# Layer 0 attention of a two-layer network on one Trainium2 core: the first steps and the loop over tiles issued in written order, with the weight rounding's loads in buffers of their own

## The chip, the cores and the metric

The kernel runs on one core of one Trainium2 chip. A core has a tensor engine for matmuls (PE, which loads the stationary operand through a side queue, PEld), a vector engine (DVE), a scalar engine (ACT), a third elementwise engine (POOL, GpSimd) and a queue that only issues transfers (SP). Each takes its instructions strictly in the order of its own queue and waits for the others by semaphores. The metric is the device time of one execution in microseconds (us). The kernel before took 1146.04 us, the median of three runs (1140.92 to 1151.8).

## The reference, cut to what matters

Two layers, each a cross attention and a feed-forward part, over 8 sequences of 256 tokens of width 512, so 2048 tokens, which the kernel handles as 16 tiles of 128. Only layer 0's attention is edited, and the preparation of the weights of the layer 0 feed-forward part that runs beside it. All of it is f32 until the rounding:

```python
# layer 0 attention; x is the layernormed input, k = v = ctx
Q, K, V = (einsum('bshd,hde->bshe', t, Wh) for t in (xh, kh, vh))      # 4 heads of 128
scores  = einsum('bshe,bthe->bhst', Q, K) / sqrt(hd)
A       = maximum(abs((scores * decay).sum(axis=0)), 1.0)              # summed over the batch
O       = einsum('hst,bthe->bshe', A, V)
Y       = (O - mu) / sqrt(var + GN_EPS) * gn_gamma + gn_beta
x       = x + relu(xn @ wg_w) * Y @ wo_w
# layer 0 feed-forward: weights are rounded to -1, 0, 1
def weight_quant(w):
    scale = 1.0 / clip(mean(abs(w)), EPS)
    return clip(round(w * scale), -1.0, 1.0) / scale
```

Since A sums over the whole batch, no tile of O can begin before every tile's scores are in. Since a weight's scale is a mean over the whole matrix, no piece of it can be rounded before all its pieces were summed.

## The kernel before, in words

`layer0_attention` has two loops.

The first, over `n` (21 steps), normalizes one token tile per step: `stats` (DVE mean and variance, ACT square root), `normed` (DVE reciprocal and scaling, four PE transposes into bank "t", ACT copy to xnT). Four steps behind it follows `queries` (one PE matmul with G = Wh Whᵀ per head and chunk, DVE copy to q), and a step later `scores`, which add up in four PSUM banks "s0" to "s3". `values` (four matmuls into bank "pv", ACT copy to v) comes in the first four steps. WhT and G are made ahead of the loop, with ACT copies. `ternary.add` loads one of twelve weight pieces (704 KB each for w1 and w3, 768 or 512 KB for w2) and sums its absolute values on ACT (L166) into `part`.

The second loop, over `i` (16 tiles and one step more), does per tile:

- `attended` (L348, L351): eight matmuls with A and V into po; a layernorm of it (DVE L71, L73, ACT root L75, DVE L77, L78); POOL multiplies by gamma and adds beta (L354, L355);
- `centered`: loads a tile of ctx (raw) and subtracts each head's mean (DVE L334, L335, POOL L336, L337), then writes it to vc_d for layer 1;
- `turned` of the tile before: four transposes of wy into bank "t", ACT copy to wyT (L365);
- `gated`: DVE product of relu(pw) and y (L360); `gate` of the next tile (L316): four matmuls into pw;
- `output` of the tile before: four matmuls with wo (L371), DVE add into X (L372) and its statistics (L100, L101);
- for odd tiles up to 11, two `values` blocks (L250, L255) of a later sequence; for the last two tiles the input of the feed-forward part (`ffn_input`: ACT L421 and L407, DVE L402 to L425);
- `ternary.round`: ACT turns the piece rounded in the step before into bf16 (L182), a new piece is loaded (L156), ACT adds the magic number that rounds it (L191), DVE clips it (L192). Ahead of a weight's first piece, `scale` sums `part` over the partitions with one matmul into wtot, in bank "t", and DVE makes the scale from it (L173 to L176).

Both kinds of weight loads, for `add` and for `round`, share one tag "wst" with two buffers. Of the eight PSUM banks, "s0" to "s3" serve sums, then po and pz; "pq" has two, "t" and "pv" one each.

The order of the work is not the written one: a planner orders each engine's queue from the written program by priorities and a cost model and hands out buffers as they come free; a buffer is reused after all who read it. Elsewhere in the kernel (layer 1's attention) a block under `manual_schedule` keeps the written order on the engines that it names.

In the built program the planner has put all twelve sums of weight pieces ahead of or among tile 0's and tile 1's work on ACT, rounds pieces in pairs, and put each odd tile's second value block between the two halves of the next tile's `attended`.

Of the kernel before, what the change touches and what calls it, by code (L numbers as in the profile page):

```python
# [19 lines left out]
F32 = mybir.dt.float32  # L20
# [4 lines left out]
AF = mybir.ActivationFunctionType  # L25
# [5 lines left out]
P = 128  # L31
D = 512
# [7 lines left out]
H0 = 4  # L40
# [63 lines left out]
def transpose_blocks(g, pool, src, n, dtype, ident, tag):  # L104

    pt = pool.tile([P, n, P], dtype, tag=tag, name="pt")
    for k in range(n):
        g.nc.tensor.transpose(pt[:, k, :], src[:, k * P : (k + 1) * P], ident)
    return pt
# [22 lines left out]
class TernaryWeights:  # L132
# [5 lines left out]
    def __init__(self, g, pool, stage, ps):  # L138
        self.g, self.stage, self.ps = g, stage, ps
        g.wq, g.iw = [], g.const.tile([P, 3], F32, tag="iw", name="iw")  # L140
        self.pieces, self.sc = [], []
        for n, (src, kb, cols) in enumerate(((g.w1T, KD, FF), (g.w3T, KD, FF), (g.w2T, NF, D))):
            g.wq.append(pool.tile([P, kb, cols], BF16, tag=f"wq{n}", name=f"wq{n}"))
            step = self.COLS // cols
            of = [(n, src, a, min(a + step, kb), cols) for a in range(0, kb, step)]
            self.pieces.append(of)
            self.sc.append(g.const.tile([P, 1], F32, tag=f"wsc{n}", name=f"wsc{n}"))
        self.part = stage.tile([P, 3, KD], F32, tag="wpart", name="wpart", bufs=1)
        g.nc.vector.memset(self.part, 0.0)
        self.to_add = [(p, m) for of in self.pieces for m, p in enumerate(of)]  # L150
        self.to_round = list(self.to_add)
        self.clipped = []

    def load(self, n, src, a, z, cols):
        w = self.stage.tile([P, self.COLS], F32, tag="wst", name="wst", bufs=2)[:, : (z - a) * cols]
        self.g.nc.sync.dma_start(  # L156
            out=w.rearrange("p (k f) -> p k f", f=cols), in_=src.rearrange("(k p) f -> p k f", p=P)[:, a:z]
        )
        return w

    def add(self):

        if self.to_add:
            piece, m = self.to_add.pop(0)
            w = self.load(*piece)
            self.g.nc.scalar.activation(w, w, AF.Abs, accum_out=self.part[:, piece[0], m : m + 1])  # L166

    def scale(self, n):
        nc, g = self.g.nc, self.g
        tot = self.ps.tile([P, KD], F32, tag="t", name="wtot", bufs=1)  # L170
        nc.tensor.matmul(tot, lhsT=g.ones[:, :P], rhs=self.part[:, n], start=True, stop=True)
        mean = g.small.tile([P, 1], F32, tag="wmean", name="wmean")
        nc.vector.tensor_reduce(mean, tot, AX.X, ALU.add)  # L173
        nc.vector.tensor_scalar(mean, mean, 1.0 / (D * FF), 1e-5, ALU.mult, ALU.max)
        nc.vector.reciprocal(self.sc[n], mean)
        nc.vector.reciprocal(g.iw[:, n : n + 1], self.sc[n])  # L176

    def round(self):

        nc, g = self.g.nc, self.g  # L180
        for (n, _, a, z, _), w in self.clipped:
            nc.scalar.activation(  # L182
                g.wq[n][:, a:z].rearrange("p k f -> p (k f)"), w, AF.Identity, bias=g.eps["-magic"]
            )
        self.clipped = []
        if self.to_round:
            piece, m = self.to_round.pop(0)
            if m == 0:
                self.scale(piece[0])
            w = self.load(*piece)  # L190
            nc.scalar.activation(w, w, AF.Identity, bias=g.eps["magic"], scale=self.sc[piece[0]])  # L191
            nc.vector.tensor_scalar(w, w, MAGIC - 1.0, MAGIC + 1.0, ALU.max, ALU.min)  # L192
            self.clipped = [(piece, w)]


def layer0_attention(g, tc, cp, qpool):
# [7 lines left out]
    with ExitStack() as ctx:  # L204
# [28 lines left out]

        WhT = work.tile([P, H0, HD0], F32, tag="wyT", name="WhT")
        nc.scalar.copy(WhT, transpose_blocks(g, ps, Wh.rearrange("p h e -> p (h e)"), H0, F32, g.ident, "t"))
        pG = ps.tile([P, H0, HD0], F32, tag="pv", name="pG")
        for h in range(H0):
            nc.tensor.matmul(pG[:, h], lhsT=WhT[:, h], rhs=WhT[:, h], start=True, stop=True)  # L240
        G = wp.tile([P, H0, HD0], F32, tag="G", name="G")
        nc.scalar.copy(G, pG)

        V = {}

        def values(b, j):
            c, o = divmod(b * S + j * P, CH)
            pv = ps.tile([P, D], F32, tag="pv", name="pv")
            for h in range(H0):
                nc.tensor.matmul(  # L250
                    pv[:, h * HD0 : (h + 1) * HD0], lhsT=g.ctxT[c][:, h, o : o + P], rhs=Wh[:, h, :],
                    start=True, stop=True,
                )
            vj = work.tile([P, D], F32, tag=f"v{j}", name=f"v{j}")
            nc.scalar.copy(vj, pv)  # L255
            V.setdefault(b, []).append(vj)
# [8 lines left out]
        for h in range(H0):  # L265
            nc.tensor.matmul(sums[h], lhsT=zero[:, :P], rhs=zero, start=True, stop=False)
# [28 lines left out]

        of, q = {0: stats(0)}, {}
        for n in range(NT + H0 + 1):
            if n + 1 < NT:  # L300
                of[n + 1] = stats(n + 1)
            if n < NT:
                normed(n, *of.pop(n))
            if 0 <= n - H0 < NT:
                q[n - H0] = queries(*divmod(n - H0, H0))
            if 0 <= n - H0 - 1:
                scores(*divmod(n - H0 - 1, H0), q.pop(n - H0 - 1))
            if n < 4:
                values(*divmod(n, 2))
            elif n >= 6:  # L310
                ternary.add()
        def gate(i):
            c, o = divmod(i * P, CH)
            pw = ps.tile([P, D], F32, tag="pq", name="pw", bufs=2)
            for k in range(KD):
                nc.tensor.matmul(  # L316
                    pw, lhsT=xnT[c][:, k, o : o + P], rhs=wg[:, k, :], start=k == 0, stop=k == KD - 1
                )
            return pw

        pw = gate(0)
        for h in range(H0):
            nc.vector.tensor_mul(AT[h], sums[h], AT[h])
            nc.scalar.activation(AT[h], AT[h], AF.Abs)
            nc.vector.tensor_scalar(AT[h], AT[h], 1.0, None, ALU.max)

        def centered(i):


            raw = work.tile([P, D], F32, tag="raw", name="raw")  # L330
            nc.sync.dma_start(out=raw, in_=g.ctx[i * P : (i + 1) * P, :])
# [26 lines left out]
        def gated(pw, y):  # L358
            wy = work.tile([P, D], F32, tag="wy", name="wy")
            nc.vector.scalar_tensor_tensor(wy, pw, 0.0, y, ALU.max, ALU.mult)  # L360
            return wy

        def turned(wy):
            wyT = work.tile([P, KD, P], F32, tag="wyT", name="wyT")
            nc.scalar.copy(wyT, transpose_blocks(g, ps, wy, KD, F32, g.ident, "t"))  # L365
            return wyT
# [6 lines left out]
            norm_stats(g, g.mv[:, i, :], g.X[i])  # L373


        wy = {}
        for i in range(NT + 1):
            if i < NT:
                y = attended(i)
                centered(i)  # L380
            if i:
                wyT = turned(wy.pop(i - 1))
            if i < NT:
                wy[i] = gated(pw, y)
            if i + 1 < NT:
                pw = gate(i + 1)
            if i:
                output(i - 1, wyT)
            if NT - 2 <= i < NT:
                g.begun.append(ffn_turned(g, *ffn_input(g, work, i - NT + 2)))  # L390
            if i % 2 and i // 2 + 2 < B:
                for j in range(2):
                    values(i // 2 + 2, j)
            ternary.round()


def quantize(g, out, tmp, x):
# [1108 lines left out]
```

## Time and profile before

| what | value |
|---|---|
| median of three runs | 1146.04 us (1140.92 to 1151.8) |
| profiled execution, its own time | 1145.64 us |
| its span | 1143.8 us |
| PE / DVE / ACT / POOL busy | 1033.5 / 545.4 / 413.3 / 375.8 us |
| layer 0 attention, last output matmul ends | 238.5 us |
| PE busy in 0:20, 60:80, 120:140 us | 12.38, 13.87, 14.81 us |
| PE busy in 140:220 us | 80.00 us |
| granted PE clock, mean | 0.969 |

The span is from the first to the last instruction of one profiled execution; the time also holds what lies around it, 1.8 us here. Busy time is the union of an engine's instructions. A row of the timeline reads: start, duration, engine, line, operation, output tile and input tiles with shape, how many instructions are merged in the row, and in brackets how long the engine had been idle and what ended that idle time. An f32 matmul stands in the trace as two passes, so "x8" is four matmuls. Names are the program's tiles with the buffer number left out.

### The profile page before, as it was taken

To read this page: it belongs to the slowest core of one execution; us is meant where nothing else is said; L and a number is where in the kernel's file an instruction comes from. 1 tells how busy PE (TensorE), PEld (TensorE's weight loads), DVE (VectorE), ACT (ScalarE), POOL (GpSimd) and SP (SyncE) were. 2 spreads that over 40 slices of the span, in tenths; PEclk is the share of its full clock that TensorE was granted. 3 is DMA by queue.
4 is the path that set the end of the run, shared out by engine and by line. 5 is a ranking of instruction groups with operands and counts; after the bars stand their busy time and mean duration, and the time that the engine had idled before them with its cause. 6 is when DMAs were issued, how large, how long until landed. Compare 5 with 4: busy or idle time off the path is not lost. (4 is left out here: it accounts for less than half of the span.)

```text
span 1143.8 us, 14661 instructions
## 1 busy us (share of the span) xinstructions
PE 1033.5 (90%) x5207; PEld 617.6 (54%) x5222; DVE 545.4 (48%) x1443; ACT 413.3 (36%) x701; POOL 375.8 (33%) x347
## 2 busy tenths in 40 slices
PE   7979899989999688998898989999999999999994
PEld 5746466534444254555534435555556666667672
DVE  6545645568888637988836941121221121221210
ACT  4445424155675357578641002112122222111111
POOL 0144422220000001354651033444454555444422
PEclk9989899999999799899899989999999999999997
DMA  9776311023323111221022345767777777888872
GB/s 350 266 262 219 127 56 46 5 50 64 58 52 65 47 34 42 71 72 57 37 96 61 138 149 151 182 171 182 180 190 191 196 197 201 208 227 230 222 186 35
DMA packets 100483, 153.65 MB, mean 134 GB/s; under 512 B 38600, under 2 KB 41288, under 8 KB 100376
## 3 DMA queue, kind: packets, MB, share of 16 engines
q1 hardware_dynamic: 81488, 106.94, 30.2%
q0 software_dynamic: 18672, 45.58, 18.2%
q8 instruction: 43, 0.70, 0.3%
q14 instruction: 40, 0.33, 0.1%
q10 hardware_dynamic: 240, 0.10, 0.0%
HBM read 111.24 MB, written 33.49 MB: 127 GB/s over the span
## 5 line engine op out<-in xcount | busy, mean ns | idle before, releaser
L1314 POOL DMA_INDIRECT out_x<-eo,to x84 | 129.8, 1545 | 226.9 <-ACT eo L1340 212.0
L1254 PE MATMUL pg<-xT,w 128*128 128x288 f32 (+7 forms) x512 | 140.3, 417 | 3.9 <-DVE xT L1311 3.9
L1270 PE MATMUL po<-w,act 128*128 128x512 f32 (+3 forms) x448 | 139.6, 494 | 4.3 <-DVE act L1259 3.9
L1254 PE MATMUL pu<-xT,w 128*128 128x288 f32 (+7 forms) x512 | 136.7, 410 | 0.0
L1340 ACT ACTIVATE eo<-po,slotw 128x512 f32<-128x512 f32 (+3 forms) x112 | 64.5, 581 | 159.2 <-PE po L1270 156.8
L1258 ACT ACTIVATE sg<-pg 128x288 f32<-128x288 f32 (+8 forms) x68 | 29.0, 427 | 257.1 <-PE pg L1254 251.7
L1254 PEld LDWEIGHTS pg<-xT,w 128*128 128x128 f32 x512 | 95.3, 191 | 33.9 <-DVE xT L1311 7.2
L1254 PEld LDWEIGHTS pu<-xT,w 128*128 128x128 f32 x512 | 97.2, 190 | 29.1 <-issue 3.0
L1311 DVE COPY xT<-pt 128x512 f32<-128x512 f32 (+3 forms) x84 | 48.8, 618 | 132.8 <-PE pt L1310 118.3
L1305 DVE SCALAR_TENSOR_TENSOR of<-xg,is_rank 128x32 f32<-128x32 f32 (+3 forms) x84 | 15.8, 188 | 188.8 <-DMA xg<-h_d,tok_of 188.2
L1295 POOL DMA_INDIRECT xg<-h_d,tok_of x84 | 82.6, 983 | 64.9 <-DVE act L1259 37.0
L1270 PEld LDWEIGHTS po<-w,act 128*128 128x128 f32 (+3 forms) x448 | 55.5, 161 | 79.8 <-issue 50.0
L556 PE MATMUL p<-wq,xqT 128*128 128x512 bf16 (+1 forms) x379 | 79.5, 361 | 3.0 <-DMA xqT<-xq 2.0
L754 DVE SCALAR_TENSOR_TENSOR ct<-pqk,xe 128x768 f32<-128x768 f32 x64 | 58.3, 950 | 25.3 <-ACT xe L731 11.8
L316 PE MATMUL pw<-wg,xnT 128*128 128x512 f32 x128 | 61.5, 626 | 0.0
L556 PEld LDWEIGHTS <-xqT 128*128 128x128 bf16 x384 | 36.7, 98 | 44.1 <-DMA xqT<-xq 6.3
L371 PE MATMUL pz<-wo,wyT 128*128 128x512 f32 x128 | 57.8, 594 | 1.4 <-ACT wyT L365 1.4
L1310 PE MATMUL pt<-ident,xg 128*128 128x128 f32 (+4 forms) x336 | 46.0, 269 | 11.6 <-DVE xT L1311 10.0
L731 ACT ACTIVATE xe<-pd 128x512 f32<-128x512 f32 x96 | 54.1, 599 | 4.9 <-PE pd L727 4.6
L1259 DVE TENSOR_TENSOR act<-pu,sg 128x288 f32<-128x288 f32 (+8 forms) x68 | 32.0, 475 | 42.8 <-PE pu L1254 42.1
L1310 PEld LDWEIGHTS pt<-ident,xg 128*128 128x128 f32 (+4 forms) x336 | 35.0, 140 | 31.3 <-issue 17.5
L812 POOL TENSOR_TENSOR hid<-hid,rsq 128x1024 f32<-128x1024 f32 x8 | 15.3, 1913 | 105.3 <-PE pqk L750 79.2
(287 smaller groups left out, 1704.9 us busy)
## 6 DMA issues: line engine op xcount, KB each, us to landing
w<-in_w SPq DMA_DIRECT2D x32, 1024.0 KB
w<-in_w SPq DMA_DIRECT2D x32, 512.0 KB
wst<-in_w1T SPq DMA_DIRECT2D x8, 704.0 KB
wst<-in_w3T SPq DMA_DIRECT2D x8, 704.0 KB
wst<-in_w2T SPq DMA_DIRECT2D x6, 768.0 KB
x<-in_x SPq DMA_DIRECT2D x16, 256.0 KB
ctxT<-in_ctxT_d SPq DMA_DIRECT2D x4, 1024.0 KB
raw<-in_ctx SPq DMA_DIRECT2D x16, 256.0 KB
```

The lines of the kernel that those rows point to most:

```text
L316: nc.tensor.matmul(pw, lhsT=xnT[c][:, k, o : o + P], rhs=wg[:, k, :], start=k == 0, stop=k == KD - 1)
L371: nc.tensor.matmul(pz, lhsT=wyT[:, k, :], rhs=wo[:, k, :], start=k == 0, stop=k == KD - 1)
L556: nc.tensor.matmul(pp[:, : z - a], lhsT=xqT[:, k, :], rhs=w[:, k, a:z], start=k == 0, stop=k == KD - 1)
L731: nc.scalar.activation(out, pd, AF.Exp)
L754: nc.vector.scalar_tensor_tensor(ct[:, r : r + 2, :], pqk[:, :, : S + P], 1.0 / math.sqrt(HD1), xe[:, r : r + 2, :], ALU.mult, ALU.mult,)
L1254: nc.tensor.matmul(pp[:, :n], lhsT=w[:, k, cols], rhs=xT[:, k, :n], start=k == 0, stop=k == KD - 1)
L1270: nc.tensor.matmul(po[h * n : (h + 1) * n, :cols], lhsT=act[:, m, j * P : j * P + n], rhs=w[:, m, h * cols : (h + 1) * cols], start=m == 0 ...
L1295: nc.gpsimd.indirect_dma_start(out=xg[:n], out_offset=None, in_=h_d, in_offset=bass.IndirectOffsetOnAxis(ap=g.tok_of[:n, r, j : j + 1], ax ...
L1310: nc.tensor.transpose(pt[:, k, :n], xg[:n, k * P : (k + 1) * P], g.ident[:n, :n])
L1311: nc.vector.tensor_copy(xT, pt[:, :, :n])
L1314: return nc.gpsimd.indirect_dma_start(out=g.out, out_offset=bass.IndirectOffsetOnAxis(ap=rows, axis=0), in_=eo, in_offset=None, compute_op ...
L1340: nc.scalar.activation(eo[:n, at : at + cols], po, AF.Copy, scale=w[:n, j : j + 1])
```

## The change

`TernaryWeights`: `add` and `round` are spread over steps, and each has a buffer of its own (tags "wadd" and "wround", one each, in place of two shared ones). `add` sums the piece that an earlier call loaded, then loads the next. A new `finish` turns the last rounded piece into bf16 and then loads the next into the same buffer; `round` makes the scale where needed and rounds the piece that `finish` loaded. wtot is a slice of a "pv" tile.

`layer0_attention`: WhT's copy moves from ACT to DVE; the zeroing of the sums, the first two `stats`, WhT and G come in a function `begin`; `begin` and the first seven steps are issued in written order on PE, ACT and DVE. `values` come in steps 3 to 6, `ternary.add` in steps 12, 14, 16, 18 and 20 alone, and goes on in the second loop. There each tile is a function `tile` under `manual_schedule` for all five queues; raw is loaded one tile ahead; `finish` stands behind `attended`, `add` behind `gated`, `round` between `gate` and `output`; the last tile's `output` comes after the loop.

```diff
-    def load(self, n, src, a, z, cols):
-        w = self.stage.tile([P, self.COLS], F32, tag="wst", name="wst", bufs=2)[:, : (z - a) * cols]
+    def load(self, tag, n, src, a, z, cols):
+        w = self.stage.tile([P, self.COLS], F32, tag=tag, name=tag, bufs=1)[:, : (z - a) * cols]
...
     def add(self):
+        if self.added:
+            (n, *_), m, w = self.added
+            self.g.nc.scalar.activation(w, w, AF.Abs, accum_out=self.part[:, n, m : m + 1])
+        self.added = None
         if self.to_add:
             piece, m = self.to_add.pop(0)
-            w = self.load(*piece)
-            self.g.nc.scalar.activation(w, w, AF.Abs, accum_out=self.part[:, piece[0], m : m + 1])
+            self.added = piece, m, self.load("wadd", *piece)
...
-        tot = self.ps.tile([P, KD], F32, tag="t", name="wtot", bufs=1)
+        tot = self.ps.tile([P, D], F32, tag="pv", name="wtot", bufs=1)[:, :KD]
...
-    def round(self):
+    def finish(self):
         nc, g = self.g.nc, self.g
-        for (n, _, a, z, _), w in self.clipped:
+        if self.rounded:
+            (n, _, a, z, _), m, w = self.rounded
             nc.scalar.activation(
                 g.wq[n][:, a:z].rearrange("p k f -> p (k f)"), w, AF.Identity, bias=g.eps["-magic"]
             )
-        self.clipped = []
+        self.rounded = None
         if self.to_round:
             piece, m = self.to_round.pop(0)
+            self.rounded = piece, m, self.load("wround", *piece)
+
+    def round(self):
+        nc, g = self.g.nc, self.g
+        if self.rounded:
+            (n, *_), m, w = self.rounded
             if m == 0:
-                self.scale(piece[0])
-            w = self.load(*piece)
-            nc.scalar.activation(w, w, AF.Identity, bias=g.eps["magic"], scale=self.sc[piece[0]])
+                self.scale(n)
+            nc.scalar.activation(w, w, AF.Identity, bias=g.eps["magic"], scale=self.sc[n])
             nc.vector.tensor_scalar(w, w, MAGIC - 1.0, MAGIC + 1.0, ALU.max, ALU.min)
-            self.clipped = [(piece, w)]
...
+        def begin():
+            for h in range(H0):
+                nc.tensor.matmul(sums[h], lhsT=zero[:, :P], rhs=zero, start=True, stop=False)
+            of[0] = stats(0)
+            nc.vector.tensor_copy(WhT, transpose_blocks(g, ps, Wh.rearrange("p h e -> p (h e)"), H0, F32, g.ident, "t"))
+            for h in range(H0):
+                nc.tensor.matmul(pG[:, h], lhsT=WhT[:, h], rhs=WhT[:, h], start=True, stop=True)
+            of[1] = stats(1)
+            nc.scalar.copy(G, pG)
...
-            if n < 4:
-                values(*divmod(n, 2))
-            elif n >= 6:
+            if 3 <= n < 7:
+                values(*divmod(n - 3, 2))
+            elif n >= NT - 4 and n % 2 == 0:
                 ternary.add()
+        with tc.manual_schedule(engines={E_.PE, E_.Activation, E_.DVE}):
+            begin()
+            for n in range(7):
+                tokens(n)
+        for n in range(7, NT + H0 + 1):
+            tokens(n)
...
-        for i in range(NT + 1):
-            if i < NT:
-                y = attended(i)
-                centered(i)
+        def tile(i, pw):
+            y = attended(i)
+            ternary.finish()
+            centered(i)
+            if i + 1 < NT:
+                loaded(i + 1)
             if i:
                 wyT = turned(wy.pop(i - 1))
-            if i < NT:
-                wy[i] = gated(pw, y)
+            wy[i] = gated(pw, y)
+            ternary.add()
             if i + 1 < NT:
                 pw = gate(i + 1)
+            ternary.round()
             if i:
                 output(i - 1, wyT)
-            if NT - 2 <= i < NT:
+            if NT - 2 <= i:
                 g.begun.append(ffn_turned(g, *ffn_input(g, work, i - NT + 2)))
             if i % 2 and i // 2 + 2 < B:
                 for j in range(2):
                     values(i // 2 + 2, j)
-            ternary.round()
+            return pw
+
+        loaded(0)
+        with tc.manual_schedule(engines={E_.PE, E_.Activation, E_.DVE, E_.Pool, E_.SP}):
+            for i in range(NT):
+                pw = tile(i, pw)
+        output(NT - 1, turned(wy.pop(NT - 1)))
```

More of the change, by code (lines that the diff above doesn't have):

```diff
@@ L151, in __init__ @@
         self.to_round = list(self.to_add)
-        self.clipped = []
-    def load(self, n, src, a, z, cols):
-        w = self.stage.tile([P, self.COLS], F32, tag="wst", name="wst", bufs=2)[:, : (z - a) * cols]
+        self.added = self.rounded = None
+    def load(self, tag, n, src, a, z, cols):
+        w = self.stage.tile([P, self.COLS], F32, tag=tag, name=tag, bufs=1)[:, : (z - a) * cols]
         self.g.nc.sync.dma_start(
@@ L184, in round @@
             )
-        self.clipped = []
+        self.rounded = None
         if self.to_round:
             piece, m = self.to_round.pop(0)
+            self.rounded = piece, m, self.load("wround", *piece)
[3 more added lines that the diff above has]
+            (n, *_), m, w = self.rounded
             if m == 0:
-                self.scale(piece[0])
-            w = self.load(*piece)
-            nc.scalar.activation(w, w, AF.Identity, bias=g.eps["magic"], scale=self.sc[piece[0]])
+                self.scale(n)
+            nc.scalar.activation(w, w, AF.Identity, bias=g.eps["magic"], scale=self.sc[n])
             nc.vector.tensor_scalar(w, w, MAGIC - 1.0, MAGIC + 1.0, ALU.max, ALU.min)
-            self.clipped = [(piece, w)]
 def layer0_attention(g, tc, cp, qpool):
@@ L232, in layer0_attention @@
         ternary = TernaryWeights(g, qpool, work, ps)
+        E_ = mybir.EngineType
         WhT = work.tile([P, H0, HD0], F32, tag="wyT", name="WhT")
-        nc.scalar.copy(WhT, transpose_blocks(g, ps, Wh.rearrange("p h e -> p (h e)"), H0, F32, g.ident, "t"))
+        G = wp.tile([P, H0, HD0], F32, tag="G", name="G")
         pG = ps.tile([P, H0, HD0], F32, tag="pv", name="pG")
[L239 to L242, printed above, removed]
         V = {}
@@ L264, in layer0_attention @@
         sums = [ps.tile([P, S + P], F32, tag=f"s{h}", name=f"s{h}") for h in range(H0)]
-        for h in range(H0):
-            nc.tensor.matmul(sums[h], lhsT=zero[:, :P], rhs=zero, start=True, stop=False)
         def stats(i):
@@ L294, in scores, with tokens @@
                 nc.tensor.matmul(sums[h][:, S:], lhsT=k[:, P:], rhs=q[:, o + P : o + S], start=False, stop=last)
-        of, q = {0: stats(0)}, {}
-        for n in range(NT + H0 + 1):
-            if n + 1 < NT:
+        of, q = {}, {}
+        def begin():
[7 more added lines that the diff above has]
+            nc.scalar.copy(G, pG)
+        def tokens(n):
+            if 1 <= n and n + 1 < NT:
                 of[n + 1] = stats(n + 1)
@@ L325, in layer0_attention, with loaded @@
             nc.vector.tensor_scalar(AT[h], AT[h], 1.0, None, ALU.max)
+        raws = {}
+        def loaded(i):
+            raws[i] = work.tile([P, D], F32, tag="raw", name="raw")
+            nc.sync.dma_start(out=raws[i], in_=g.ctx[i * P : (i + 1) * P, :])
         def centered(i):
-            raw = work.tile([P, D], F32, tag="raw", name="raw")
-            nc.sync.dma_start(out=raw, in_=g.ctx[i * P : (i + 1) * P, :])
+            raw = raws.pop(i)
             by_head = raw.rearrange("p (h d) -> p h d", d=HD1)
```

## The prediction

> **What bounds the kernel now.** Only layer 0's attention is edited; its last matmul group ends at 238.5 us of the 1143.8 us span. By program order, every instruction after that stage stands as before, so the question is where in these 238.5 us the tensor engine (PE) stands still, and what the new order makes it wait for. I first cut the stage into stretches (columns: stretch, its length, then busy us and instruction count of PE, its weight loads, DVE, ACT, POOL; granted clock; DMA share; GB/s):
>
> ```profile
> 71.50:77.80 6.30, 0.21 (x2) 0.01 (x1) 2.34 (x7) 3.34 (x5) 3.07 (x3) 0.90 0.64 238
> 77.80:84.50 6.70, 6.66 (x13) 3.32 (x14) 2.57 (x10) 3.40 (x6) 5.67 (x8) 0.58 0.78 263
> 84.50:121.60 37.10, 36.55 (x167) 22.97 (x165) 19.35 (x40) 16.26 (x18) 17.63 (x24) 1.00 0.59 201
> 121.60:127.00 5.40, 0.21 (x3) 0.02 (x2) 3.04 (x8) 0.00 (x0) 3.35 (x6) 0.75 0.26 85
> 177.00:225.00 48.00, 48.00 (x210) 29.35 (x209) 23.30 (x47) 12.98 (x20) 12.64 (x10) 1.00 0.07 24
> ```
>
> PE is full from 84.5 to 121.6 and in 177 to 225; two holes stand out, and behind the first the clock is 0.58. The timeline names them:
>
> ```profile
> 77.84 1.11 PE L108 MATMUL pt<-ident,wy 128*128 128x128 f32 x4 [6.13 <-DVE wmean L174]
> 126.99 1.11 PE L108 MATMUL pt<-ident,wy 128*128 128x128 f32 x4 [5.19 <-DVE wmean L173]
> ```
>
> Both holes end at the weights' total. The second is what it says: the transposes share bank "t" with wtot, whose reading on DVE stood behind reads of raw that waited for DMA. The first has another root: tile 0's square root (L75) ran only at 73.00, because ACT was standing in L166 for loads. PE full otherwise means that a gain can come only from holes: 6.13 + 5.19, the half clock behind them (gate's eight passes took 5.91 and 5.23 against 3.60, so 2.3 + 1.6, transposes 0.5 each), together **16.2 us**, and the start.
>
> **The change, part by part.** Times below are of the profiled execution (1145.64 us; the median of the runs shown is 1146.04, so the same base within 0.4).
>
> *Start.* WhT goes from ACT, where it ran at 8.76 behind square roots that waited for x, to DVE, where the transposes of Wh (3.78 + 1.09) and one stats let it end near 6.1. That brings G's matmuls from 9.38 to about 6.1, 3.3 us. But the steps are then in written order, and from step 4 each tile's transposes need, after the previous query matmul, DVE's q copy 0.69, stats 0.69, aggregate and reciprocal 0.3, xn 0.55: 2.2 us, while PE has only 0.9 (values) to 2.2 (values and scores). Followed step by step, PE waits some 1.4 and 1.2 us in steps 5 and 6, and step 8's transposes come at 28.7 against 29.24. Ends: 0 to 3.3 us gained. I take 0.5, since the x rows limit both. Attended tile 0 then ends at 65.6 (before: 66.1).
>
> *Tile 0 and the bank.* The root now stands ahead of ACT's load-bound work. From the end of attended, rows 149.16 to 154.31 give 5.15 to the gated product, then four wtot operations 0.6, ACT's round 1.6, clip 0.8, po's stats 0.88, the next root 0.2 and conversion 1.47: conversion C1 ends at 77.0, output 0 starts 0.55 later at 77.55 against 84.49. So **6.9 us ahead**, most of the first hole. The total in "pv" costs nothing: its matmuls (0.14) stand behind a value copy long done, and the next values come after an output of 3.4 us; without that cover 0.6 us each, three times.
>
> *The loop's new wait.* Rounding has one buffer of its own, and one load per tile may start only when the previous piece is converted. In written order ACT does: root, conversion, wyT, abs, round (waits for the load), value copies; DVE does: clip, x add, stats of x, **then** stats of the next po, which the next root and conversion need. So a load's landing sits on a cycle from conversion to conversion, and output's wyT copy is behind the conversion. What a load takes, the rows show where ACT's idle ended at a landing; each load was issued as an engine let its buffer go (SP issues two in each of these rows; the second ones at 46.24 and 95.10):
>
> ```profile
> 44.88 1.69 SPq L156 DMA_DIRECT2D wst<-in_w1T  x2
> 92.93 2.50 SPq L156 DMA_DIRECT2D wst<-in_w1T  x2
> ```
> ```profile
> 49.15 1.38 ACT L166 ACTIVATE wst<-wst 128x1408 f32<-128x1408 f32 x1 [0.45 <-DMA wst<-in_w1T]
> 93.62 1.46 ACT L182 ACTIVATE wq<-wst,eps_-magic 128x1408 bf16<-128x1408 f32 x1
> 97.79 1.56 ACT L191 ACTIVATE wst<-wst,eps_magic,wsc 128x1408 f32<-128x1408 f32 x1 [2.71 <-DMA wst<-in_w1T]
> ```
>
> 44.88 to 49.15 is 4.27, 92.93 to 97.79 is 4.86; others are 4.57 (53.95 to 58.52), 4.59 (174.70 to 179.29), 4.84 (50.64 to 55.48), and 5.31 with a second load and a write beside it (81.60 to 86.91). I take **4.6**, the middle of the loads that went alone. DVE's part is contiguous in
>
> ```profile
> 189.09 0.68 DVE L372 TENSOR_TENSOR x<-pz,x 128x512 f32<-128x512 f32 x1
> 189.80 0.69 DVE L100 BATCH_NORM_STATS2 st<-x 128x6 f32<-128x512 f32 x1
> 190.53 0.18 DVE L101 BATCH_NORM_AGGREGATE mv<-st 128x2 f32<-128x6 f32 x1
> 190.63 0.67 DVE L71 BATCH_NORM_STATS2 st<-po 128x6 f32<-128x512 f32 x1
> 191.33 0.18 DVE L73 BATCH_NORM_AGGREGATE mv<-st 128x2 f32<-128x6 f32 x1
> ```
>
> that is 1.54 to po's stats and 0.88 for them. Even tile: load 4.6, round 1.60, clip 0.80, 1.54, 0.88, root 0.23, conversion 1.47 = **11.1**, against 9.1 of PE work. Odd tiles also make two value blocks; they now stand side by side in one bank, the first copy queued behind the round on ACT: load 4.6, round 1.47, copy 0.58, second values 0.99, attended 1.78, hop 0.20, 0.88, 0.23, 1.47 = **12.2**, against 10.9. From C1 to C12 there are six odd and five even: 73.2 + 55.5 = 128.7, and the four larger pieces (w2T: round, clip, conversion 0.3 more) 1.2: 129.9. So C12 = 206.9, output 11 starts at 207.45 against 204.15: **3.3 us behind**; the 6.9 and the second hole are spent. The moves of raw (loaded a tile early, its POOL work behind y's, its load on SP ahead of wadd's) lie off this cycle, in DVE's wait for POOL; if a raw came late, DVE's old waits for it, 0.7 to 2.0 us, would add to it.
>
> *Tail.* Tile 14's ffn_input is now whole on DVE ahead of tile 15's po stats. From output 13's end: hop 0.2, x add to aggregate 1.54, two small 0.3, ACT xn 0.91, absolute maximum, scale and reciprocal 1.15, ACT quantize 0.82, xq and scale 0.58 = 5.5, against 1.98 before (225.77 to 227.75): **3.4 us later**, as PE has only 5.7 us of other work there, and output 14's wyT is behind the same root. That hole is some 4.8 us, like the 5.19 that was followed by half clock: between 0 and 2.3, I take 1.
>
> **Sum:** +3.3 + 3.4 + 1 = 7.7 beside the 238.5, all later stages moving with it: 1153.4, said as **1154**.
>
> [...]
>
> **Rivals.** *Slower loads:* each landing at 4.86 to 5.5, as where vc_d writes or wadd run beside it: 11 x 0.26 to 0.9 more, so 1157 to 1164. For it: 81.60; against: in the new order vc_d's packets and wadd come after the round's load.
> *Not slower:* the landing never binds. Place: ACT's round; price: PE alone then needs 111.0 from output 0 to 11 (five pairs of 20.01 and 10.92) and 0.83 more in each of six odd tiles for the value copy, 116.0; output 11 at 193.6, 10.6 ahead, tail 4.4: 1139.4. It decides below a load of 4.6 - 7.7/11 = 3.9 us; the shortest row is 4.27.
> *The start does what its 3.3 us say*, or the tail is covered: 1147 to 1151.
> *The order is not obeyed* can be put aside: the built queues of all five engines stand as described.
>
> **Numbers.** Forecast 0.47 (1150 to 1158.5; a third of that over the bound), slower loads 0.32, not slower 0.15 (0.08 of it with the start's other 2.8 and without the tail's 3.4, at 1133), start or tail 0.06. One per cent is 11.5 us, about what a measurement of this kernel tells from no change (runs 1140.9 to 1151.8). Over 1157.5: 0.15 + 0.32 = 0.47; under 1134.6: 0.08; between 0.45. Range 1140 to 1164 takes in loads of 3.9 to 5.4 us.
>
> **What would show it.** Right: no 5 to 6 us hole at wtot; ACT's round with idle ended by wround's DMA in tiles 1 to 11; outputs waiting 1 to 2 us for wyT; pairs of tiles at 23.3 us until the pieces end, 20 to 21 after; a hole of 4 to 5 us ahead of output 14. Wrong: pairs near 20.8 while pieces are rounded, or loads landing under 4 us.

## The result, and the profile after

| | before | after |
|---|---|---|
| median, beside the prediction | 1144.39 us (1140.92 to 1151.8, four runs) | 1158.13 us (1154.58 to 1162.52, four runs) |
| ratio after to before | | 1.0114, 95% interval 1.0079 to 1.015 |
| the same kernels again, later | 1147.21 us (1140.02 to 1153.23) | 1159.12 us (1147.63 to 1160.38) |
| ratio | | 1.008, 95% interval 1.0049 to 1.011 |
| profiled execution, span | 1143.8 us | 1160.6 us |

So the change costs about 1 per cent; the forecast was 1154 in a range of 1140 to 1164. The same stretches as before, now of the changed kernel (columns: stretch, its length, then busy us and count of PE, its weight loads, DVE, ACT, POOL; granted clock; DMA share; GB/s):

```profile
71.50:77.80 6.30, 5.48 (x25) 3.02 (x23) 3.27 (x10) 2.27 (x3) 2.94 (x4) 1.00 0.36 143
77.80:84.50 6.70, 4.59 (x16) 2.49 (x16) 2.72 (x4) 4.37 (x6) 4.25 (x5) 1.00 0.69 218
84.50:121.60 37.10, 34.70 (x158) 21.78 (x159) 22.03 (x42) 17.36 (x22) 12.70 (x15) 1.00 0.50 177
121.60:127.00 5.40, 4.74 (x12) 1.95 (x11) 3.35 (x7) 3.60 (x5) 3.48 (x3) 1.00 0.41 132
177.00:225.00 48.00, 45.61 (x198) 27.61 (x197) 28.03 (x52) 12.65 (x19) 18.71 (x22) 1.00 0.23 77
```

Both big holes are gone (5.48 of 6.30 and 4.74 of 5.40 busy, at full clock), but no stretch is full any more: 34.70 of 37.10 where before had 36.55, 45.61 of 48.00 where before had 48.00. The timeline of the changed kernel's PE names the new waits (start, us, engine, line, operation, and in brackets the idle time ahead and what ended it):

```profile
73.31 0.66 PE L108 MATMUL pt<-ident,wy 128*128 128x128 f32 x4 [0.43 <-DVE wy L388]
79.26 3.70 PE L399 MATMUL pz<-wo,wyT 128*128 128x512 f32 x8 [1.86 <-ACT wyT L393]
85.00 1.16 PE L256 MATMUL pv<-Wh,ctxT 128*128 128x128 f32 x8 [1.14 <-ACT v L261]
...
235.13 5.40 PE L399 MATMUL pz<-wo,wyT 128*128 128x512 f32 x8 [4.90 <-ACT wyT L393]
```

The waits of 6.13 and 5.19 us became six for wyT and six for v, of 0.66 to 1.86 us each, between output 0 and output 11, and one of 4.90 in the tail. Output 0 starts at 79.26 (before: 84.49, 5.2 ahead), output 11 at 206.23 (204.15, 2.1 behind), output 15 at 241.64 (234.97, 6.7 behind), the feed-forward part at 245.4 (238.5, 6.9 behind), the context matmuls L515 at 259.0 (249.1, 10.0 behind).

The cycle itself, in one even tile of the changed kernel, by the timelines of SP's queue, ACT and DVE:

```profile
113.01 0.33 SPq L156 DMA_DIRECT2D wround<-in_w3T  x1
...
111.53 1.45 ACT L186 ACTIVATE wq<-wround,eps_-magic 128x1408 bf16<-128x1408 f32 x1
117.14 1.56 ACT L201 ACTIVATE wround<-wround,eps_magic,wsc 128x1408 f32<-128x1408 f32 x1 [2.21 <-DMA wround<-in_w3T]
122.21 1.45 ACT L186 ACTIVATE wq<-wround,eps_-magic 128x1408 bf16<-128x1408 f32 x1
...
118.74 0.89 DVE L202 TENSOR_SCALAR wround<-wround 128x1408 f32<-128x1408 f32 x1 [1.99 <-ACT wround L201]
119.55 0.68 DVE L400 TENSOR_TENSOR x<-pz,x 128x512 f32<-128x512 f32 x1
120.26 0.69 DVE L100 BATCH_NORM_STATS2 st<-x 128x6 f32<-128x512 f32 x1
120.99 0.18 DVE L101 BATCH_NORM_AGGREGATE mv<-st 128x2 f32<-128x6 f32 x1
121.09 0.67 DVE L71 BATCH_NORM_STATS2 st<-po 128x6 f32<-128x512 f32 x1
```

The conversion ends at 112.98, the next load is issued at once, ACT stands 2.21 us for its landing, and clip, x add, both statistics and the root follow without a gap to the next conversion: 10.68 us, against 9.1 of PE work. From the end of a conversion, with the load issued 0.03 us behind it, to the next round it took 4.10 to 4.20 us for 704 KB (4.53 once), 4.57 to 4.72 for 768 KB, 3.92 for 512 KB.

### The profile page after: what moved, and what is told of

It is laid out like the page before. It is cut to its first block, busy times and chain, and to the rows that moved or that the text cites. A ratio compares the mean times of both kernels' runs of the same rounds, so it can differ in the third digit from the quotient of the medians.

```text
span 1160.6 us, 14665 instructions
## 1 busy us (share of the span) xinstructions
PE 1040.4 (90%) x5207; PEld 620.2 (53%) x5222; DVE 554.3 (48%) x1444; ACT 412.6 (36%) x700; POOL 373.3 (32%) x347
## 4 chain that ended last, share of the span: by engine, by line
PE 52%; DVE 13%; DMA 12%; ACT 9%; issue 7%; POOL 4%; POOLq 0%; DVEq 0%; SPq 0%; ACTq 0%
PE po L1309 10%; PE pg L1293 8%; PE pu L1293 8%; PE p L595 3%; DMA xg<-h_d,tok_of 3%; DMA out_x<-eo,to 2%; POOL out_x L1353 2%; DMA hqT<-hq 2%; PE pt L1349 2%; ACT wround L201 2%; DVE xT L1350 2%; DMA wround<-in_w2T 1%; DMA wround<-in_w3T 1%; ACT wq L186 1%; PE pz L399 1%
## 5 line engine op out<-in xcount | busy, mean ns | idle before, releaser
L382 POOL TENSOR_TENSOR y<-y,gam 128x512 f32<-128x512 f32 x16 | 20.2, 1265 | 164.1 <-DVE y L78 164.1
L399 PE MATMUL pz<-wo,wyT 128*128 128x512 f32 x128 | 60.2, 615 | 13.4 <-ACT wyT L393 13.4
L339 PE MATMUL pw<-wg,xnT 128*128 128x512 f32 x128 | 57.6, 592 | 0.0
```

Source lines behind the costliest of these rows:

```text
L339: nc.tensor.matmul(pw, lhsT=xnT[c][:, k, o : o + P], rhs=wg[:, k, :], start=k == 0, stop=k == KD - 1)
L399: nc.tensor.matmul(pz, lhsT=wyT[:, k, :], rhs=wo[:, k, :], start=k == 0, stop=k == KD - 1)
```

## The experiments

The kernel before was measured beside each of them, and ratios are to it. The changed kernel was measured beside some of them alone ("the same kernels again" in the table), so gains over it are read from the ratios, against 1.008 and 1.0114, and from the profiles. Half clock means that the granted clock of the tensor engine in the profile is 0.50.

**Two buffers for the rounding's loads.**

```diff
-        if self.to_round:
+        while self.to_round and len(self.ahead) < 2:
             piece, m = self.to_round.pop(0)
-            self.rounded = piece, m, self.load("wround", *piece)
+            self.ahead.append((piece, m, self.load("wround", *piece, bufs=2)))
+        if self.ahead:
+            self.rounded = self.ahead.pop(0)
```

> The changed kernel, with two buffers for the rounding's loads, so that each piece is asked for a whole tile before it is rounded (room for the second buffer comes from sharing: G in raw's buffers, the zeros in xq's, the query copies in wyT's, the gated product in place of y). Theory (the landing of a single buffer's load sits on the cycle from conversion to conversion): ACT's idle of about 2 us ahead of each round goes, pairs of tiles fall from 22.45 to about 21, the time from output 0 to output 11 from 127.0 to some 116 (five pairs of 20.0, one tile of 10.9, six value copies of 0.83), so about 11 us less: 1147. Rival (the written order on ACT and DVE sets the cycle, the landing only fills a gap in it): pairs stay above 22, under 3 us less: 1155 to 1158.

Measured 1143.93 us (1138.84 to 1147.47), ratio 0.9949 (0.9918 to 0.998). ACT of this kernel:

```profile
94.45 1.55 ACT L204 ACTIVATE wround<-wround,eps_magic,wsc 128x1408 f32<-128x1408 f32 x1
100.15 0.29 ACT L75 ACTIVATE sd<-mv,eps_gn 128x1 f32<-128x1 f32 x1 [4.14 <-DVE mv L73]
...
103.55 1.55 ACT L204 ACTIVATE wround<-wround,eps_magic,wsc 128x1408 f32<-128x1408 f32 x1
```

No round waits for a landing any more, and PE's waits for wyT in the loop are gone but for 0.16 at output 4, 0.49 at output 8 and the 1.86 ahead of output 0. One pair of tiles, here and in the changed kernel (columns as above):

```profile
93.80:114.80 21.00, 20.32 (x91) 12.48 (x90) 12.89 (x23) 11.15 (x15) 9.76 (x11) 1.00 0.56 192
```
```profile
91.70:114.20 22.50, 20.60 (x92) 12.41 (x90) 12.41 (x22) 11.27 (x15) 8.55 (x11) 1.00 0.52 179
```

Output 0 to 11 took 119.8 in place of 127.0: 7.2 less, not 11. Of the 3.8 missing, output 0 at half clock (5.40 in place of 3.70) makes 1.7, and pairs of tiles of 20.9 to 21.7 us make 2.0, where the expectation with its value copies stood for 20.8. The theory holds: the single buffer's landing set the loop, and pairs fell below the 22 of the rival.

By the ratios the whole gain is 15 to 19 us, and the rest of it has other sources. With the shared buffers lg lies elsewhere: POOL filled it at 235.37 without a wait (see the run on lg below), Wkv waited for nothing, and that is 3.3 us of the 8.6 by which the context matmuls came earlier than in the changed kernel. The half-clock stretch behind the feed-forward part was 10.24 us in place of 23.89, worth 4.4 (see the last section). Where the remainder lies is open.

**A second load behind each.**

```diff
             self.rounded = piece, m, self.load("wround", *piece)
+            self.load("decoy", *piece)
```

> The changed kernel with a second load of the same piece, into a buffer that nobody reads, issued right behind each of the rounding's loads (room as in the run with two buffers). Theory (each microsecond of the landing stands once in each tile's cycle): by the row of before where two loads and a write went together, 5.31 us in place of 4.15, the landing is some 1.2 us later, ACT's idle ahead of the round 3.3 to 3.5 us in place of 2.2 to 2.3, both kinds of tile longer by the same amount, output 0 to output 11 about 13 us more than 127.0, the kernel near 1172. Rival (the first load has the queue to itself until it has landed, or other work covers it): under 3 us more.

Measured 1156.63 us (1152.94 to 1157.41), ratio 1.0075 (1.0043 to 1.0107). SP's queue and ACT:

```profile
101.22 0.33 SPq L156 DMA_DIRECT2D wround<-in_w1T  x1
101.60 0.42 SPq L156 DMA_DIRECT2D decoy<-in_w1T  x1
...
105.30 1.56 ACT L202 ACTIVATE wround<-wround,eps_magic,wsc 128x1408 f32<-128x1408 f32 x1 [2.26 <-DMA wround<-in_w1T]
```

For 704 KB, issue to round was 4.03 to 4.15 us in six tiles and 4.47 in one, against 4.07 to 4.17 and once 4.50 in the changed kernel: a second load of the same size issued 0.4 us later on the same queue did not slow the first. Output 0 to 11 took 128.8, of which up to 1.7 is a half-clock stretch at 177.0. The theory failed: a load issued behind the piece did not delay it. The prediction's rival "slower loads" had fallen with the landings of the changed kernel itself. In this kernel too, as its buffers are shared, POOL filled lg without a wait, so its time lacks the 3.3 us of the run on lg below.

**The value blocks apart.**

```diff
             ternary.round()
+            if i % 2 and i // 2 + 2 < B:
+                values(i // 2 + 2, 0)
             if i:
                 output(i - 1, wyT)
...
-                for j in range(2):
-                    values(i // 2 + 2, j)
+                values(i // 2 + 2, 1)
```

> The changed kernel with the two value blocks of an odd tile apart: the first between the round and the output, the second where both stood. Theory (in odd tiles the copy behind the round on ACT, 0.58, and the second block's 0.99 lie on the cycle from conversion to conversion ahead of the next attended): odd tiles 10.7 to 10.9 in place of 11.8, PE's waits of about 1.1 us for v go, six times 1: output 11 some 5 to 6 us earlier, 1152 to 1154. Rival (the landing absorbs it, since PE's wait only moves to the output's wyT): under 1.5 us.

Measured 1163.8 us (1156.04 to 1168.01), ratio 1.0139 (1.007 to 1.0208): no gain, in a wide interval. PE and ACT:

```profile
106.41 1.16 PE L256 MATMUL pv<-Wh,ctxT 128*128 128x128 f32 x8 [1.92 <-ACT v L261]
...
104.33 1.56 ACT L201 ACTIVATE wround<-wround,eps_magic,wsc 128x1408 f32<-128x1408 f32 x1 [2.23 <-DMA wround<-in_w1T]
105.80 0.56 ACT L261 COPY v<-pv 128x512 f32<-128x512 f32 x1
```

The first block is made early, but its copy still stands behind the round on ACT, and the round behind the landing. PE's wait only changed place: for v from 6.8 to 11.7 us in all, for wyT from 13.4 to 8.1. Conversions are still 11.74 apart in an odd tile (98.81 to 110.55). Output 0 to 11 took 129.4 against 127.0, with two half-clock stretches of 3.41 us inside that the changed kernel's profile has not; they can be worth up to 3.4, so at best 1 us was gained here, and the rival holds.

**The two early feed-forward inputs behind the last output.**

```diff
-            if NT - 2 <= i:
-                g.begun.append(ffn_turned(g, *ffn_input(g, work, i - NT + 2)))
...
         output(NT - 1, turned(wy.pop(NT - 1)))
+        for j in range(2):
+            g.begun.append(ffn_turned(g, *ffn_input(g, work, j)))
```

> The changed kernel, with the two early feed-forward inputs written behind the last output, out of the block in written order, so that the planner places them. Theory: the 4.9 us hole ahead of output 14 and the half clock behind it go (output 15 at 237 in place of 241.6, 4.6 less), and since xq of the second input is then made before the loop's last adds, POOL reaches the transfers of Wif sooner, and the 3.3 us that DVE's Wkv adds go too: 5 to 8 us less, 1150 to 1153. Rival (the same DVE work only moves behind the last outputs and delays the feed-forward part's start as much): 0 to 2 us less.

Measured 1148.89 us (1146.57 to 1152.68), ratio 1.0019 (0.9989 to 1.0049). From output 13 to output 15 the changed kernel took 17.2 us, this one 13.2, the kernel before 12.6: the tail's 4 us are shown. The second half of the theory fell: the second xq and the start of the feed-forward part both came some 3 us earlier, so that Wkv still waited 3.28 us for Wif. By the ratios the gain is 7 to 11 us. Up to the context matmuls the profile has 3.1 of them, and its half-clock stretch behind the feed-forward part is 13.65 us in place of 23.89, 4.4 more (see the last section). The ten runs were granted a clock of 0.971 to 0.980, the changed kernel's later ten 0.966 to 0.975; whether the order of the work makes that is not shown.

**lg behind Wif.** This run is about something that the prediction had not looked at. POOL and DVE of the changed kernel:

```profile
247.20 0.58 POOL L1252 MEMSET lg<- 128x576 f32 x1 [5.53 <-DVE turn L711]
249.34 1.04 POOL L489 DMA_DIRECT2D Wif<-in_Wf  x1
...
254.46 0.29 DVE L491 TENSOR_TENSOR Wkv<-Wif 128x128 f32<-128x128 f32 x1 [3.61 <-DMA Wif<-in_Wf]
```

and POOL of the kernel before:

```profile
236.49 0.58 POOL L1213 MEMSET lg<- 128x576 f32 x1 [3.69 <-DMA xqT<-xq]
...
239.94 1.05 POOL L450 DMA_DIRECT2D Wif<-in_Wf  x1
```

lg lies in memory that layer 0's attention used, so its filling waits for the last reader, and POOL issues Wif's transfers behind it. In the kernel before, in the changed kernel and with the inputs behind, lg's filling began 2.63, 2.67 and 2.67 us after DVE had made the second xq, so it is the late second xq that made it 10.7 us later. DVE stood for Wif with PE's h products behind it, and PE waited 1.69 and 1.29 us for h.

```diff
-        self.Wkv = wp.tile([P, KD, 2 * H1], F32, tag="Wkv", name="Wkv")
+        self.Wkv = wp.tile([P, KD, 2 * H1], F32, tag="Wkv", name="Wkv"); nc.gpsimd.memset(g.lg, NONE)
...
-    nc.gpsimd.memset(g.lg, NONE)
```

> The changed kernel, with POOL's filling of lg (whose memory is that of layer 0's attention, so that it waits for the last feed-forward input) put behind the two transfers of Wif; on the other engines only DVE's Wkv stands one place earlier. Theory (lg's wait of 5.5 us holds Wif's transfers, Wkv then holds DVE for 3.6 us and with it PE): Wif is issued near 241.5, Wkv waits under 0.5 us, context matmuls at 255.7 in place of 259.0, 3.3 us less. Rival (Wif's landing is late for another reason, or the next wait takes its place): under 1 us less.

Measured 1154.03 us (1150.25 to 1159.01), ratio 1.0041 (1.0008 to 1.0074). DVE of this kernel:

```profile
252.91 0.28 DVE L491 TENSOR_TENSOR Wkv<-Wif 128x128 f32<-128x128 f32 x1
```

Wif was issued at 243.72 and 244.93, Wkv waited for nothing, and between output 15 and the context matmuls nothing was lost against before (9.47 and 9.46 us behind; in the changed kernel 6.67 and 9.96). The 3.3 us are this wait. The forecast of 255.7 for the context matmuls was missed, at 258.54: this execution came to output 15 2.8 us later than the changed kernel's, by half-clock stretches from 177.7 on and behind the hole ahead of output 14. By the ratios the gain is 4 to 8 us, of which 3.3 are traced to the edit.

**The bank alone, on the kernel before.**

```diff
-        tot = self.ps.tile([P, KD], F32, tag="t", name="wtot", bufs=1)
+        tot = self.ps.tile([P, D], F32, tag="pv", name="wtot", bufs=1)[:, :KD]
```

> The kernel before with one line of the change: the weights' total in bank pv in place of t; the queues of all engines stand as before. Theory (the second hole of 5.19 us is the shared bank, the first, 6.13 us, is the square root that stands behind loads on ACT): the second hole and the half clock behind it go, the first stays: about 7 us less than the kernel before, 1138. Rival (DVE itself stands in the read of raw that waits for its load, and the product gated, behind it on DVE, holds PE a step later): under 2 us.

Measured 1147.53 us (1142.43 to 1151.67), ratio 0.9985 (0.9951 to 1.002). PE and DVE:

```profile
101.47 0.63 PE L108 MATMUL pt<-ident,wy 128*128 128x128 f32 x4 [0.87 <-DVE wy L360]
107.56 3.70 PE L371 MATMUL pz<-wo,wyT 128*128 128x512 f32 x8 [2.03 <-ACT wyT L365]
128.56 1.09 PE L108 MATMUL pt<-ident,wy 128*128 128x128 f32 x4 [3.76 <-DVE wy L360]
...
119.41 0.69 DVE L334 TENSOR_REDUCE mean<-raw 128x16 f32<-128x512 f32 x1 [3.60 <-DMA raw<-in_ctx]
```

The first hole stays (5.01 us); the second became 3.76 us under another name, with 0.87 and 2.03 new ahead of it: the product wy stands on the same DVE, behind the same reads of raw. DVE of the kernel before:

```profile
123.17 0.69 DVE L360 SCALAR_TENSOR_TENSOR wy<-pw,y 128x512 f32<-128x512 f32 x1 [2.72 <-POOL y L355]
126.78 0.15 DVE L173 TENSOR_REDUCE wmean<-wtot 128x1 f32<-128x4 f32 x1
```

There the product was ready at 123.86 and the bank did hold the transposes for the last 3.1 us, to 126.99; with the bank free, raw landed later and the product itself was ready only at 128.42. So taking the bank away alone gains nothing.

**The bank and earlier raws, on the kernel before.**

```diff
-            raw = work.tile([P, D], F32, tag="raw", name="raw")
+            raw = work.tile([P, D], F32, tag="raw", name="raw", bufs=4)
```

> The kernel before, in the planner's order, with the total in bank pv and four buffers for raw in place of two, so that a tile of ctx may be loaded up to three tiles early (room from the query copies in wyT's buffers and the gated product in place of y). With the bank alone the second hole only changed its name: PE then stood 0.87, 2.03 and 3.76 us for gated products that DVE made behind reads of raw. Theory (the root of the second hole is raw's late landing): these three waits fall below 1 us together, output 4 starts 4 to 6 us earlier than 132.96, and the kernel is 5 to 8 us under the kernel before, about 1140. Rival (raw is read no earlier, or the weight loads come later for it and ACT's rounds hold DVE): under 2 us.

Measured 1145.76 us (1136.43 to 1147.94), ratio 0.9979 (0.9949 to 1.001). No wait of 2 us is left after 108 us, but waits of 3.13, 2.72, 0.63 and 2.10 us stand before it, with ACT idle up to 6.73 us for weight pieces, and output 4 starts at 132.05 in place of 132.96. With the bank free and raw early, nothing holds PE at 121.8 any more: from the end of tile 0's attended to output 4 it took 60.7 us in place of 66.9. But that end came at 71.3 in place of 66.1, as PE had waited 1.68, 1.05 and 1.18 us for DVE in the last queries and scores, with ACT idle 3.24, 2.79 and 3.96 us for weight pieces, so the gain was lost ahead of it. The planner's order differs there, and four buffers for raw with the bank in place were not tried. In the planner's order neither hole was to be had by one cause.

**The bank back, in the changed kernel.**

```diff
-        tot = self.ps.tile([P, D], F32, tag="pv", name="wtot", bufs=1)[:, :KD]
+        tot = self.ps.tile([P, KD], F32, tag="t", name="wtot", bufs=1)
```

> The changed kernel with the weights' total back in bank t. Theory (in the written order the total stands between gate and output and DVE reads it at once, so that no transposes are held): no difference, 1157 to 1160, and no new wait over 0.5 us on PE in the three tiles with a total. Rival (the transposes of the next tile wait for DVE's read): 1 to 2 us in each of three tiles, 1161 to 1165.

Measured 1161.09 us (1157.21 to 1161.6), ratio 1.0117 (1.008 to 1.0153); the largest new wait is 0.49 us. In the written order the bank makes no difference that was measured.

**The first steps left to the planner, and the changed kernel again.**

```diff
-        with tc.manual_schedule(engines={E_.PE, E_.Activation, E_.DVE}):
-            begin()
-            for n in range(7):
-                tokens(n)
-        for n in range(7, NT + H0 + 1):
+        begin()
+        for n in range(NT + H0 + 1):
             tokens(n)
```

> The changed kernel without its order of the first steps: begin and all 21 steps are left to the planner, the loop over tiles stays in written order. Theory (the written order makes the start 1.2 us longer, since PE stands 1.43 and 1.11 us for DVE's xn and statistics): attended of tile 0 ends near 66.1 in place of 67.3, the rest moves with it, 1 to 2 us less in all. Rival (the x rows' landing limits both): under 0.5 us of difference there.

Measured 1154.97 us (1146.84 to 1157.11), ratio 1.0059 (1.003 to 1.0089), against 1.008 (1.0049 to 1.011) for the changed kernel beside it: 2 to 4 us less, within overlapping intervals. Attended of tile 0 ended at 66.51 here, 0.8 and 1.8 us ahead of the two profiles of the changed kernel (67.28 and 68.27).

The changed kernel without any edit:

> The changed kernel itself, measured and profiled again beside the next three. In the six profiles so far the half-clock stretch between the layer 0 feed-forward part and layer 1's attention, behind a hole of 10.92 us that all of them have, lasted 17.07, 23.89, 10.24, 10.24, 13.65 and 23.89 us. Theory (its length is drawn anew in each execution, so it belongs to the spread of the runs and not to the change): the time is again 1.0 to 1.3 per cent above the kernel before, the stage ends again 6 to 8 us later than before and the context matmuls 10 us, and the stretch has another length. Rival (the changed order makes it long): 23.89 again.

Measured 1159.12 us (1147.63 to 1160.38), ratio 1.008 (1.0049 to 1.011). The theory fell on the stretch: it was 23.89 us again, as the rival had it, though the rival's cause is not shown (see the last section). Output 15 was 8.2 us behind the kernel before, the context matmuls 11.5.

In all profiles together, attended of tile 0 ended at 65.0, 66.1, 66.5 and 67.4 in four with the planner's start (without the run with four raw buffers, whose order there differs: 71.3), and at 66.5 to 68.5 (mean 67.5) in nine with the written one: some 1.3 us later, with overlapping spreads.

**All together.** The edits of four runs above in one kernel (two buffers, the inputs behind the last output, lg behind Wif, the blocks apart); a second version adds the diff that leaves the start to the planner.

> The changed kernel with all of it: two buffers for the rounding's loads, the feed-forward inputs behind the last output, lg behind Wif, the value blocks apart. If the losses that these removed one by one add up (14 us, 9 us, 2 us of the Wif wait that the second left, and 4 us for PE's waits of 0.68 in six odd tiles): about 1130, 1.5 per cent under the kernel before. If they overlap (the tail's hole and Wif's wait are both made by the loop's lateness): 1138 to 1142.

> The version with two buffers, the feed-forward inputs behind the last output, lg behind Wif and the value blocks apart (1132.77), with begin and all first steps left to the planner. If the written start costs 1 to 2 us by itself: 1131; the same within 3 us in any case.

Measured 1132.77 us (1129.76 to 1139.94), ratio 0.9878 (0.9815 to 0.9941), and 1136.06 us (1135.83 to 1136.28), ratio 0.9909 (0.9878 to 0.9939): the same within their intervals, and both under both kernels. The first one's pairs of tiles:

```profile
78.70:98.70 20.00, 20.00 (x88) 12.34 (x89) 13.44 (x23) 12.31 (x17) 11.06 (x12) 1.00 0.57 208
98.70:118.90 20.20, 20.20 (x92) 12.55 (x92) 13.21 (x28) 10.61 (x14) 8.33 (x10) 1.00 0.56 193
```

PE is busy all the time from output 0 to output 11, 110.4 us in place of 127.0. No wait for v is left in this stretch, where the run with two buffers had six of 0.68 us. The blocks apart, worth 1 us at best while the landing set the cycle, take these waits away once it does not.

## Why the prediction was right, and where it was not

- **The holes at the total.** They went, as said. Their causes were half right: the run with the bank alone shows that the second hole was not the shared bank's alone, since it came back as a wait for the product behind raw.
- **The start.** Forecast 0.5 us ahead, measured 1.2 behind in the profile, 1.3 by the means above. The waits in steps 5 and 6 are there (1.43 and 1.11 against 1.4 and 1.2), but PE also stood three times 0.68 us for xnT in the first steps, where four transposes took 1.1 us each time (0.6 later). So step 8's transposes came at 31.23 and not at 28.7, and output 0 was 5.2 ahead, not 6.9. From tile 0's attended to the first conversion the sum was right (11.4, measured 11.46); it holds the gated product's own 0.69 beside the terms that it lists.
- **The loop.** The mechanism is shown by the two buffers. The term mis-sized is the load: 4.6 forecast, 4.10 to 4.20 measured for 704 KB. With 4.15 the same sums give 10.65 and 11.75 for even and odd tiles; measured were 10.63 and 10.68 (11.05 with the one load of 4.53) and 11.77 to 11.87. C1 to C12 took 126.1 against 129.9. Of the six rows read for it, four had a second weight load issued within 2.2 us and two (4.57 and 4.84) had none; why loads took longer in the kernel before is not shown, and the run with a second load speaks against a load issued behind. The four w2T pieces are three larger and one smaller, not four larger.
- **The rival "not slower".** Its bound of 3.9 us for the load is where loss and gain of the whole sum cancel, not where the landing stops to bind. By the same sums it binds down to 2.6 us in an even tile and 3.3 in an odd one (11.1 against 9.1 and 12.2 against 10.9), so measured loads of 4.15 had to show.
- **Luck in the sum.** At output 11 the forecast of 3.3 us behind against the measured 2.1 looks close, but a loop over by 3.8 stands against a start under by 1.7 and 0.8 more from the last conversion to output 11, for which the forecast had 0.55 and which took 1.38.
- **The tail.** Forecast 3.4 + 1 (its terms, 5.5 less 1.98, make 3.5), measured 4.6. Output 14 took 5.40 us in place of 3.60 to 3.70: 1.7 to 1.8 of half clock.
- **"All later stages moving with it."** This step failed: 3.3 us were lost behind the stage, by POOL's wait for lg ahead of Wif. The prediction put this at nothing because every instruction there stands as before; the order did, the moment at which memory came free did not.
- **The rest.** The stage and Wif make 10.0 of the 16.8 us between the two profiles. Some 3 more are the clock stretch below; the remaining 3 to 4 are open. The two ratios, 1.0114 and 1.008, stand for 9 to 13 us.

So the stage itself was forecast at 7.7 us and took 6.7; the forecast of 1154 was under by an unseen loss of 3.3 and by clock.

## What to carry to other kernels

When an order is written out by hand, look for a buffer whose next load is issued by the last step of the work that it feeds: here the whole landing (4.10 to 4.20 us for 704 KB) was then a term of the cycle, on an engine that looks half idle (ACT was busy 17.36 of 37.10 us), and a second buffer took it out. A wait with a name on it is not its cause: ask what the named engine would do next if that wait were gone, before pricing the hole. And follow every in-order queue past the end of the edited stage, where memory is handed on: here a fill of memory that the edited stage had used waited 5.53 us and held the loads behind it, at a cost of 3.3 us.

## What the runs showed of the hardware

Between the layer 0 feed-forward part and layer 1's attention every profile has a PE hole of 10.42 or 10.43 us (the 10.92 in the expectation above counts it somewhat longer), and behind it a stretch at half clock of very different length (10.24 to 23.89 us), for the same order of work too (17.07 in the kernel before, 23.89 with the bank alone). Its length went with when in the hole the clock fell:

| from the hole's start to the fall, us | stretch at half clock, us | from the hole's start to the first score matmul of layer 1, us | profiles |
|---|---|---|---|
| 2.05 | 13.65 | 25.3 | inputs behind |
| 2.09 | 17.07 | 26.6 | before |
| 2.8 to 4.8 | 23.89 | 29.2 to 29.7 | ten, the changed kernel twice among them |
| 5.0, 5.1 | 10.24 | 25.3, 25.2 | lg behind Wif; two buffers |

All lengths are 3, 4, 5 or 7 times 3.41 us, and the same matmuls came up to 4.5 us later by them. The first transposes behind it, in the kernel before and in the changed one:

```profile
395.50 1.11 PE L584 MATMUL ft<-ident,xn 128*128 128x128 f32 x4 [10.43 <-ACT xn L581]
```
```profile
405.78 1.11 PE L623 MATMUL ft<-ident,xn 128*128 128x128 f32 x4 [10.43 <-ACT xn L620]
```

and the clock of the ten us from 410 on in the changed kernel, with PE busy 7.98 of 10.00 us and the clock still at half:

```profile
410.00:420.00 10.00, 7.98 (x34) 5.26 (x33) 0.00 (x0) 3.75 (x5) 0.00 (x0) 0.50 0.16 58
```

What ended the stretch is not shown. In the changed kernel it lasted from 399.43 to 423.32 us. In its seven parts of 3.41 us PE was busy for 0, 0.48, 2.69, 2.74, 2.73, 2.75 and, in the last, 3.15 us; four waits of 0.67 to 0.72 us for copies on ACT lie in between. In the kernel before (387.17 to 404.24) PE was busy in the five parts for 0, 0, 1.23, 2.85 and 2.96 us. In both the last part is the busiest, but PE's busy time alone did not decide: from 474.52 to 481.35 us of the changed kernel PE was busy throughout, and the clock stayed at half for these 6.83 us.

This one place moved the work behind it by up to 4.5 us, 0.4% of the time. So one of these profiles against another can be off by that much without any difference in the work. Whether the changed order favours the long stretch (both its own profiles had it) stays open.
